# Attention over kept tokens on one core: reordering ScalarE's squares and sums, VectorE's bias and the length reductions

## The chip, the cores and the metric

The kernel runs on one core of one Trainium2 chip. The core has five engines, which run in parallel, each through its own queue in order: TensorE (PE in the profile; PEld is its weight load), VectorE (DVE), ScalarE (ACT), GpSimd (POOL) and SyncE (SP, which only issues DMAs here). Times are device microseconds (us) of whole executions; for each kernel the median of several runs is given. One further execution is profiled; its span runs from the first to the last instruction.

## The reference

A residual attention over 8 batches of 512 features by 1024 tokens in float32, with a mask of zeros and ones per token and the same projection for queries, keys and values:

```python
xt = jnp.transpose(x, (0, 2, 1))
q = xt @ Wq.T
qh = q.reshape(B, T, NH, dk).transpose(0, 2, 1, 3)          # 8 heads of 64
scores = scale * jnp.einsum('bhqd,bhkd->bhqk', qh, qh)
logits = (scores * cmask + (1.0 - cmask) * NEG) * rmask      # masked keys: NEG; masked queries: all 0
attn = jax.nn.softmax(logits, axis=-1)
ctx = jnp.einsum('bhqk,bhkd->bhqd', attn, qh)
out = x + transpose(ctx.reshape(B, T, D) @ Wo.T)
```

A masked key gets no weight, and a masked query attends to all tokens alike, so its context is the mean over tokens. About half of the tokens are kept.

## The kernel before

**What it computes on.** The kernel gathers the kept tokens of a batch (at most 543 of 1024) into 544 columns, the last of which (NK - 1) holds the mean token. Attention runs over these columns alone. Afterwards a gather by rank hands each token its row: its own, or that of the mean.

**Pairs and slots.** The order is written out by hand. The outer loop goes over 32 pairs (b, pr): batch b, and one of 4 pairs of heads. Each pair has five slots, k = 0 to 4, one for each chunk of 128 keys: first the short last chunk (64 rows, tile `el`), then chunks 0 to 3 (tile `e`). Each engine meets the work of a slot in the order in which the loop issues it:

1. scores (L584): TensorE multiplies keys by queries into `s` (PSUM, two buffers); ScalarE takes the exponential with the column `bias` of the pair (L605). The weighted values and the sums use the result.
2. add_up (L614): VectorE sums the exponentials of the chunk before, in two instructions (L622). In slot 0 also those of the pair before, then invert (reciprocals, rows out and back by SP's DMAs); in slot 4 contexts (the pair before is scaled, L740).
3. In pr 0 and 1, for the next batch: turn (VectorE transposes x, L417; SP stores it as `xd`), add_features (ScalarE sums features, L436), mean_of, search (VectorE finds the rows to gather, L473), gather (POOL's indirect DMA).
4. fetch and finish_blocks: POOL gathers output rows of the batch before into `g`; VectorE transposes a block and adds x (L825, L828). Eight blocks a batch, from pr 2 of the next batch to pr 0 of the one after; the table FINISH gives the slots, as (pr, k).
5. The list `todo[k]` of slots_of (L885): slots 0 to 2 the weighted values of the pair before (attend_short, attend_half; ScalarE copies `cT`); in pr 2, slots 1 and 2, put_mean and collect (TensorE transposes gathered tokens into `xc`); in slot 3 bias_of for the next pair and project (`pq`, `qT`) for the pair after that; in slot 4 values for the latter; in pr 1, slots 3 and 4, the output projection (`po`) of the batch before.

**The bias.** The exponentials subtract a bound on the scores. values (L543) makes the transposed values `v`, lets ScalarE square them (`sq`, L559), and VectorE adds the squares by rows (`len`, L561, 128x640) and takes the largest (`top`, L568). bias_of (L570) transposes this column on TensorE (L574), and VectorE makes `m` (L576, L577) and `bias` (L579) of it. The first exponential of a pair, that of `el` in slot 0, waits for the bias.

**Where this stands in the profiled run.** Pair (5,3) runs on TensorE from 489.72 to 504.66 us, (6,0) to 521.27, (6,1) to 553.91 (it has the output projection of batch 5), (6,2) to 570.63. The transposes L574 for the pairs (6,0), (6,1) and (6,2) start at 498.93, 515.53 and 533.43, in slot 3 of the pair before each.

Of the kernel before, what the change touches and what calls it, by code (L numbers as in the profile page):

```python
# [12 lines left out]
AF = mybir.ActivationFunctionType  # L13
ALU = mybir.AluOpType
# [291 lines left out]
def attention_of_kept_tokens(ctx, tc, x, mask, wq, wo, out, ident, wqT, woT, verdict, flag):  # L306


    nc = tc.nc
# [197 lines left out]
    def put_mean(b):  # L507

        xcs[b] = sb.tile([P, ND, NK], F32, tag="xc", name=f"xc_{b}", bufs=1)
        pm = bank(f"mean_{b}")  # L510
        for d in range(ND):
            nc.tensor.matmul(
                pm[d * Q : (d + 1) * Q, :A], within, xmeans[b][:, d, :], start=True, stop=True
            )
        nc.vector.tensor_scalar(xcs[b][:, :, NK - 1], pm[:, :A], 1.0 / T, None, ALU.mult)


    qTs, vs, tops, biases = {}, {}, {}, {}
# [24 lines left out]
    def values(pair):  # L543
        nm = "%d_%d" % pair
        qT = qTs[pair]
        v = sb.tile([P, NC, P], F32, tag="v", name=f"v_{nm}", bufs=4)
        for at, n in ((0, LAST), (LAST, 1)):
            pt = bank(f"v_{nm}_{at}")
            for i in range(n):
                c = at + i  # L550
                nc.tensor.transpose(
                    pt[:, i * P : (i + 1) * P], qT[:, c * P : (c + 1) * P], ident
                )
            nc.scalar.copy(
                v[:, at : at + n, :], pt[:, : n * P].rearrange("p (c d) -> p c d", d=P)
            )
        vs[pair] = v
        sq = sb.tile([P, NC, P], F32, tag="sq", name=f"sq_{nm}", bufs=1)
        nc.scalar.activation(sq, v, AF.Square)  # L559
        lengths = sb.tile([P, 2 * NC], F32, tag="len", name=f"len_{nm}")  # L560
        nc.vector.tensor_reduce(  # L561
            lengths,
            sq.rearrange("p c (h d) -> p (c h) d", h=2),
            axis=AX.X,
            op=ALU.add,
        )
        tops[pair] = sb.tile([P, 1], F32, tag="top", name=f"top_{nm}")
        nc.vector.tensor_reduce(tops[pair], lengths, axis=AX.X, op=ALU.max)  # L568

    def bias_of(pair):  # L570

        b, pr = pair
        pt = bank(f"top_{b}_{pr}")
        nc.tensor.transpose(pt[:, :P], tops.pop(pair).to_broadcast([P, P]), ident)  # L574
        m = sb.tile([P, 1], F32, tag="m", name=f"m_{b}_{pr}")
        nc.vector.tensor_reduce(m, pt[:, :P], axis=AX.X, op=ALU.max)  # L576
        nc.vector.tensor_scalar(m, m, -SCALE, None, ALU.mult)  # L577
        biases[pair] = sb.tile([P, NC], F32, tag="bias", name=f"bias_{b}_{pr}")
        nc.vector.tensor_scalar(biases[pair], pens[:, b, :], m, None, ALU.add)  # L579
# [222 lines left out]

    BLOCKS = range(B - 1)

    def place_blocks():

        for a in range(A):
            for j in range(A):
                nc.vector.tensor_copy(
                    block_origin[a * Q : (a + 1) * Q, :, j::A],  # L810
                    placed[j * Q : (j + 1) * Q, :, a * (NT // A) : (a + 1) * (NT // A)],
                )
# [72 lines left out]
    def slots_of(p):  # L885

        b, pr = pairs[p]
        todo = [[] for _ in range(NC)]
        before = pairs[p - 1] if 0 < p < len(pairs) - 1 else None
        behind = pairs[p + 1] if p + 1 < len(pairs) else None  # L890
        ahead = pairs[p + 2] if p + 2 < len(pairs) else None
        if before:
            todo[0].append(lambda: attend_short(before))
            for hf in range(2):
                todo[1 + hf].append(lambda hf=hf: attend_half(before, hf))
        if p == 0:
            todo[0].append(lambda: project(behind, 1))
            todo[1].append(lambda: values(behind))
        late = p == 2
        if pr == 2 and b + 1 < B:  # L900
            at = (2, 2, 2, 3, 3) if late else (1, 2, 2, 2, 2)
            todo[at[0]].append(lambda: put_mean(b + 1))
            for i in range(NC):
                todo[at[i]].append(lambda i=i: collect(b + 1, i))
        if p == ND - 1:
            todo[3].append(lambda: values(behind))
        if behind:
            todo[4 if p == ND - 1 else 3].append(lambda: bias_of(behind))
        if ahead:
            for hf in range(2):  # L910
                todo[4 if late else 3].append(lambda hf=hf: project(ahead, hf))
        if ahead and not late:
            todo[4].append(lambda: values(ahead))
        if p == ND - 1:
            for d in range(ND):
                todo[3 + d // 2].append(lambda d=d: turn_weights(woT, "wo", d))
        if pr == 1 and b > 0:
            for i in range(NC):
                todo[(3, 3, 4, 4, 4)[i]].append(lambda i=i: output(b - 1, i))
        if p + 1 == len(pairs):  # L920
            for i in range(NC):
                todo[(1, 1, 2, 3, 4)[i]].append(lambda i=i: begin_output(b, i))
        return todo
# [148 lines left out]
    def late(n):  # L1072
# [14 lines left out]
        for hf in range(2):  # L1087
            project(pairs[0], hf)
        values(pairs[0])
        project(pairs[1], 0)  # L1090
        order = [LAST, *range(LAST)]
        bias_of(pairs[0])


        TURN = [(0, 2), (0, 4), (1, 0), (1, 1)]
        SEARCH = {(1, 0): (0, 1), (1, 1): (2,), (1, 2): (3,), (1, 3): (4,)}
        LATER = {(1, 1): (0,), (1, 2): (1,), (1, 3): (2, 3), (1, 4): (4,)}

# [1 line left out]
        GATHER_LATER = {(1, 4): (0, 1, 2), (2, 0): (3,), (2, 1): (4,)}  # L1100
        FETCH = {(2, k): (k,) for k in range(NC)} | {(3, k): (NC + k,) for k in range(NT - NC)}
        FINISH = {
            (2, 3): (0,),
            (2, 4): (1,),
            (3, 0): (2,),
            (3, 1): (3,),
            (3, 2): (4,),
            (3, 3): (5,),
            (3, 4): (6,),
            (0, 1): (7,),  # L1110
        }
        FINISH_LAST = {(3, 1): (0, 1), (3, 2): (2, 3), (3, 3): (4,)}
        for p, pair in enumerate(pairs):
            b, pr = pair
            before = pairs[p - 1] if p else None
            todo = slots_of(p)
            for k, c in enumerate(order):
                scores(pair, c)
                if k:
                    add_up(pair, order[k - 1])  # L1120
                if k == 0 and before:
                    add_up(before, order[-1])
                    if p + 1 < len(pairs):
                        invert(before)
                    else:
                        inv = inverses(before)
                if p + 1 == len(pairs):
                    if k == 1:
                        spread(before, inv)
                        contexts(before)  # L1130
                elif k == 4 and before:
                    contexts(before)
                if b + 1 < B:
                    if (pr, k) in TURN:
                        turn(b + 1, TURN.index((pr, k)))
                    if pr < 2 and pr * NC + k < NN * ND:
                        add_features(b + 1, pr * NC + k)
                    if pr == 1 and k == 3:
                        mean_of(b + 1)
                    for i in (SEARCH if b else LATER).get((pr, k), ()):  # L1140
                        search(b + 1, i)
                    if pr == 0 and k == 1:
                        queries_of(b + 1)
                    for i in (GATHER if b else GATHER_LATER).get((pr, k), ()):
                        gather(b + 1, i)
                if pr == 3 and k == 0 and b + 2 < B:
                    load_batch(b + 2)
                    load_ranks(b + 2)
                if pr == 1 and k == 2 and b > 0:
                    load_rest(b - 1)  # L1150
                if b > 0:
                    for i in FETCH.get((pr, k), ()):
                        fetch(b - 1, i)
                if p == 0 and k == 1:
                    place_all()
                if p == 1 and k == 4:
                    turn_places()
                if p == 2 and k == 2:
                    place_blocks()
                for i in (FINISH if b + 1 < B or pr == 0 else FINISH_LAST).get((pr, k), ()):  # L1160
                    of = b - 2 if pr == 0 else b - 1
                    if of in BLOCKS:
                        finish_blocks(of, i)
                for task in todo[k]:
                    task()
                issue_stores()
            if p + 2 == len(pairs):
                attend_short(pair)
                for hf in range(2):
                    attend_half(pair, hf)  # L1170
# [120 lines left out]
```

## Time and profile before

| what | before |
|---|---|
| median of 3 runs | 711.64 us (704.85 to 713.55) |
| profiled execution | 708.39 us, span 706.6 us |
| TensorE busy | 645.6 us, 91% of the span |
| VectorE busy | 532.7 us, 75% |
| ScalarE busy | 377.6 us, 53% |
| GpSimd busy | 172.9 us, 24% |
| mean granted TensorE clock | 0.963 |
| chain that ended last | DVE 40%, PE 30%, DMA 14%, issue 7% |

The profile page gives busy time per engine, the costliest groups of instructions by line, and the chain of work that ended last. A group's line reads: source line, engine, operation, tiles written and read, count, busy time and mean of one, then the engine's idle time just before such instructions and what ended it. The waits view lists the same idle time by who waited for whom; the timeline lists start, duration, engine and line. Busy shares are means over stages: an engine with a modest share may still be late for a part of each batch.

### The profile page before, as it was taken

How to read it: one execution, taken by the hardware profiler on the slowest of the kernel's cores; microseconds unless marked ns; L12 is line 12 of the kernel's file. 1: busy time of each engine (PE TensorE's matmuls, PEld its weight loads, DVE VectorE, ACT ScalarE, POOL GpSimd, SP SyncE). 2: the span in 40 equal slices, each digit the busy share in tenths (PEclk: the TensorE clock that was granted, in tenths of full speed). 3: DMA queues.
4: the chain of work that ended last, by engine and by line, in shares of the span. 5: the costliest groups of instructions: out<-in, count | busy, mean ns of one | idle time of the engine just before them, and what ended most of it. 6: DMA issues, size and time to landing. Idle time of an engine off the chain costs nothing.

```text
span 706.6 us, 12031 instructions
## 1 busy us (share of the span) xinstructions
PE 645.6 (91%) x4139; PEld 385.6 (55%) x4139; DVE 532.7 (75%) x1568; ACT 377.6 (53%) x763; POOL 172.9 (24%) x222
## 2 busy tenths in 40 slices
PE   6688799999999998999999998999899999999952
PEld 5555466546655665556555654546555565544421
DVE  5268858857998599786998499875998589837761
ACT  5477447646673567446673564646664455444300
POOL 4720201054012521054011521055010530024040
PEclk9899799999999999999999998999999999999985
DMA  8444242494468744794467744795546840764256
GB/s 289 150 166 108 83 152 66 117 246 132 169 159 191 231 142 159 188 272 151 168 163 171 226 147 151 194 255 165 188 120 181 242 139 15 188 156 120 60 181 191
DMA packets 96704, 116.42 MB, mean 165 GB/s; under 512 B 10304, under 2 KB 74304, under 8 KB 96624
## 3 DMA queue, kind: packets, MB, share of 16 engines
q1 hardware_dynamic: 79552, 74.07, 39.7%
q0 software_dynamic: 12848, 39.30, 16.7%
q10 hardware_dynamic: 4224, 2.10, 1.0%
q8 instruction: 36, 0.59, 0.4%
q14 instruction: 44, 0.36, 0.2%
HBM read 72.78 MB, written 42.65 MB: 163 GB/s over the span
## 4 chain that ended last, share of the span: by engine, by line
DVE 40%; PE 30%; DMA 14%; issue 7%; ACT 3%; SPq 2%; POOL 2%; DVEq 0%; POOLq 0%
DVE junk L622 12%; PE s L601 6%; PE po L756 6%; PE pq L529 6%; PE av L638 5%; DMA od<-oc 5%; DVE xr L828 5%; DMA xin<-xd,source 4%; DVE o L825 4%; DVE junk L473 4%; DMA g<-od,block_origin 3%; SPq L425 2%; DVE cT L740 2%; DVE xt L417 2%; DMA xd<-xt 2%
## 5 line engine op out<-in xcount | busy, mean ns | idle before, releaser
L622 DVE CUSTOM_DVE_ANT_0 junk<-e,valid 128x544 f32<-128x544 f32 x256 | 184.7, 721 | 18.3 <-ACT e L605 13.0
L601 PE MATMUL s<-qT 64*128 64x272 f32 (+1 forms) x1280 | 183.2, 425 | 16.5 <-ACT el L605 14.7
L605 ACT ACTIVATE e<-s,bias 128x544 f32<-128x544 f32 x256 | 170.1, 710 | 26.1 <-PE s L601 21.8
L601 PEld LDWEIGHTS s<-qT 64*128 64x128 f32 (+1 forms) x1280 | 93.4, 177 | 91.4 <-issue 39.5
L638 PE MATMUL av<-e,v 128*64 128x272 f32 x1024 | 135.0, 407 | 0.0
L529 PE MATMUL pq<-xc,wqT 128*128 128x272 f32 x512 | 124.9, 397 | 0.0
L529 PEld LDWEIGHTS pq<-xc,wqT 128*128 128x128 f32 x512 | 97.5, 196 | 19.1 <-issue 1.1
L756 PE MATMUL po<-woT,cT 128*128 128x512 f32 (+1 forms) x448 | 105.5, 434 | 0.0
L638 PEld LDWEIGHTS av<-e,v 128*64 128x64 f32 x1024 | 69.3, 139 | 58.8 <-issue 27.1
L485 POOL DMA_INDIRECT xin<-xd,source x40 | 42.6, 1065 | 213.1 <-DVE m L577 29.6
L756 PEld LDWEIGHTS po<-woT,cT 128*128 128x128 f32 (+1 forms) x448 | 47.8, 150 | 52.7 <-issue 51.9
L536 ACT COPY qT<-pq 128x272 f32<-128x272 f32 x64 | 24.7, 385 | 80.3 <-PE pq L529 80.3
L857 POOL DMA_INDIRECT g<-od,block_origin x56 | 56.6, 1011 | 36.9 <-DMA od<-oc 19.0
L825 DVE STREAM_TRANSPOSE o<-g 128x512 f32<-128x512 f32 x56 | 39.3, 701 | 29.2 <-DMA g<-od,block_origin 29.2
L763 ACT COPY oc<-po 128x512 f32<-128x512 f32 (+1 forms) x35 | 18.3, 522 | 76.4 <-PE po L756 76.4
L661 ACT COPY cT<-av 128x272 f32<-128x272 f32 x62 | 23.9, 385 | 59.3 <-PE av L638 59.3
L561 DVE TENSOR_REDUCE len<-sq 128x10 f32<-128x640 f32 x32 | 25.9, 808 | 31.8 <-ACT sq L559 31.8
L765 POOL DMA_DIRECT2D od<-oc x56 | 30.3, 543 | 77.1 <-ACT oc L763 59.1
L381 POOL TENSOR_SCALAR valid<-count,kept 128x544 f32<-128x544 f32 x8 | 13.1, 1642 | 144.4 <-DVE sums L700 144.3
L417 DVE STREAM_TRANSPOSE xt<-x 128x1024 f32<-128x1024 f32 x28 | 34.7, 1240 | 14.9 <-DMA xd<-xt 14.3
L473 DVE TENSOR_SCALAR_CACHE_REDUCE junk<-rank,key 128x1024 f32<-128x1024 f32 (+4 forms) x40 | 39.8, 994 | 2.6 <-ACT rank L1031 2.4
L622 DVE CUSTOM_DVE_ANT_0 junk<-el,part 128x272 f32<-128x272 f32 x64 | 29.3, 457 | 15.3 <-ACT el L605 14.2
(139 smaller groups left out, 649.5 us busy)
## 6 DMA issues: line engine op xcount, KB each, us to landing
x<-in_x_dram SPq DMA_DIRECT2D x56, 256.0 KB
xd<-xt SPq DMA_DIRECT2D x112, 128.0 KB
xr<-in_x_dram SPq DMA_DIRECT2D x28, 512.0 KB
out_dram<-xr SPq DMA_DIRECT2D x24, 512.0 KB
rb<-row SPq DMA_DIRECT2D x60, 160.0 KB
od<-oc POOLq DMA_DIRECT2D x28, 256.0 KB, 7.4
rank<-ranks SPq DMA_DIRECT2D x6, 512.0 KB
xd<-xt POOLq DMA_DIRECT2D x8, 256.0 KB, 4.5
```

Source lines behind the costliest of these rows:

```text
L417: nc.vector.transpose(xt.rearrange("p k (d f) -> p k d f", d=ND), xs[b][r][:, :, at : at + n].rearrange("p d (k t) -> p k d t", t=Q),)
L473: nc.vector.tensor_scalar(junk[:, :n], rank[:, i * P :], key[:, col], 0.0, ALU.is_le, ALU.add, accum_out=found[:, col])
L485: nc.gpsimd.indirect_dma_start(out=xin[:n, :], out_offset=None, in_=xds[b], in_offset=bass.IndirectOffsetOnAxis(ap=searches[b][2][:n, i : ...
L529: nc.tensor.matmul(pq[:, :KH], wqT[:, d, pr * P : (pr + 1) * P], xcs[b][:, d, cols], start=(d == 0), stop=(d == ND - 1),)
L601: nc.tensor.matmul(s[to, h, :KH], qT[heads[h], keys], qT[heads[h], queries], start=True, stop=True)
L605: nc.scalar.activation(e[:, hf if c < LAST else 0, :, :], s[:, :, :KH], AF.Exp, bias=biases[pair][:, c : c + 1], scale=SCALE,)
L622: nc.vector.tensor_tensor_reduce(junk[:, :n].rearrange("p (f k) -> p f k", k=KH), e[:, :, h, :], (valid if c < LAST else part).rearrange(" ...
L638: nc.tensor.matmul(av[head, :KH], v[keys, c, head], e[keys, hf if c < LAST else 0, h, :], start=(c == first), stop=(c == last),)
L756: nc.tensor.matmul(po[k * n : (k + 1) * n, :w], cTs[b, pr][:, i * P : i * P + n], woT[:, pr, k * w : (k + 1) * w], start=(pr == 0), stop=( ...
L825: nc.vector.transpose(o.rearrange("p k t -> p (k t)"), gs[b, i])
L828: nc.vector.tensor_tensor(to, o, to, ALU.add)
L857: nc.gpsimd.indirect_dma_start(out=g, out_offset=None, in_=ods[b], in_offset=bass.IndirectOffsetOnAxis(ap=block_origin[:, b, i : i + 1], a ...
```

## The change

Six edits, all of order or of engine; the arithmetic stays the same.

1. put_mean writes the mean's column of `xc` on ScalarE instead of VectorE.
2. The squares, `len` and `top` leave values and become a function lengths_of. It ran with values, in slot 4 of the pair before the one that makes the bias. Now it stands in slot 1 of the pair that makes the bias in slot 3: first in todo[1], ahead of attend_half (in the first pair in slot 2, in the fourth in slot 3).
3. bias_of is issued right after the scores of slot 3 (the fourth pair: slot 4), ahead of add_up, instead of in the todo list at the end of the slot.
4. The feature sums move from one in each of the eight slots from pr 0, k 0 to pr 1, k 2 to slots 1, 2 and 3 of pr 0 and pr 1, two of them in each slot 3; mean_of moves from slot 3 to slot 4 of pr 1.
5. finish_blocks moves one slot back for blocks 0 to 6, so that block 0 comes in slot 4 of pr 2 (it was slot 3) and block 6 in slot 0 of pr 0 (it was slot 4 of pr 3).
6. place_blocks, 16 casts of a table, is cut in two halves and moves from slot 2 of the third pair to slots 0 and 1 of the fourth.

```diff
-        nc.vector.tensor_scalar(xcs[b][:, :, NK - 1], pm[:, :A], 1.0 / T, None, ALU.mult)
+        nc.scalar.mul(xcs[b][:, :, NK - 1], pm[:, :A], 1.0 / T)
...
         vs[pair] = v
+
+    def lengths_of(pair):
+
+        nm = "%d_%d" % pair
         sq = sb.tile([P, NC, P], F32, tag="sq", name=f"sq_{nm}", bufs=1)
-        nc.scalar.activation(sq, v, AF.Square)
+        nc.scalar.activation(sq, vs[pair], AF.Square)
         lengths = sb.tile([P, 2 * NC], F32, tag="len", name=f"len_{nm}")
         nc.vector.tensor_reduce(
             lengths,
...
-    def place_blocks():
-
-        for a in range(A):
+    def place_blocks(half):
+
+        for a in range(half * A // 2, (half + 1) * A // 2):
...
+        if behind:
+            if p == 0:
+                todo[2].append(lambda: lengths_of(behind))
+            elif p != ND - 1:
+                todo[1].insert(0, lambda: lengths_of(behind))
...
         if p == ND - 1:
             todo[3].append(lambda: values(behind))
-        if behind:
-            todo[4 if p == ND - 1 else 3].append(lambda: bias_of(behind))
+            todo[3].append(lambda: lengths_of(behind))
...
         values(pairs[0])
+        lengths_of(pairs[0])
...
+        FEATURES = {(r, k): (r * G + k - 1, *((r * G + 3,) if k == 3 else ())) for r in range(NN) for k in (1, 2, 3)}
...
         FINISH = {
-            (2, 3): (0,),
-            (2, 4): (1,),
-            (3, 0): (2,),
-            (3, 1): (3,),
-            (3, 2): (4,),
-            (3, 3): (5,),
-            (3, 4): (6,),
+            (2, 4): (0,),
+            (3, 0): (1,),
+            (3, 1): (2,),
+            (3, 2): (3,),
+            (3, 3): (4,),
+            (3, 4): (5,),
+            (0, 0): (6,),
             (0, 1): (7,),
         }
...
                 scores(pair, c)
+                if k == (4 if p == ND - 1 else 3) and p + 1 < len(pairs):
+                    bias_of(pairs[p + 1])
                 if k:
                     add_up(pair, order[k - 1])
...
-                    if pr < 2 and pr * NC + k < NN * ND:
-                        add_features(b + 1, pr * NC + k)
-                    if pr == 1 and k == 3:
+                    for i in FEATURES.get((pr, k), ()):
+                        add_features(b + 1, i)
+                    if pr == 1 and k == 4:
                         mean_of(b + 1)
...
-                if p == 2 and k == 2:
-                    place_blocks()
+                if p == ND - 1 and k < 2:
+                    place_blocks(k)
```

## The prediction

> **What bounds the kernel now.** I read the page's busy shares first.
>
> ```profile
> PE 645.6 (91%) x4139; PEld 385.6 (55%) x4139; DVE 532.7 (75%) x1568; ACT 377.6 (53%) x763; POOL 172.9 (24%) x222
> ```
>
> TensorE (PE) sets the pace: 91% busy, so all the idle time that a reordering can recover is small. Next the waits of TensorE, because they are that idle time by cause (columns: total us, times, longest).
>
> ```profile
> PE s L601 <- ACT el L605: 14.7, 19, 3.3
> ...
> PE av L638 <- DVE m L576: 5.0, 4, 1.3
> PE xc L498 <- DVE xc L515: 4.6, 1, 4.6
> ...
> PE s L601 <- ACT e L605: 1.8, 1, 1.8
> ...
> PE top L574 <- DVE top L568: 0.7, 1, 0.7
> ```
>
> The four upper rows are what the change aims at: 26.1 us, 3.7% of the 706.6 us span. The last row is the one to remember: the transpose `top` of bias_of hardly ever waits for VectorE (DVE) today. Then the timelines around pairs (6,0) and (6,1), TensorE first, because VectorE's mean share of 75% hides where it is late.
>
> ```profile
> 498.93 0.32 PE L574 MATMUL top<-ident,top 128*128 128x128 f32 x1
> ...
> 508.67 0.73 PE L601 MATMUL s<-qT 64*128 64x272 f32 x4 [1.86 <-ACT el L605]
> ...
> 515.53 0.32 PE L574 MATMUL top<-ident,top 128*128 128x128 f32 x1
> ...
> 523.69 0.68 PE L638 MATMUL av<-el,v 64*64 64x272 f32 x4 [1.28 <-DVE m L576]
> ...
> 533.43 0.32 PE L574 MATMUL top<-ident,top 128*128 128x128 f32 x1
> ```
>
> VectorE over the same stretch:
>
> ```profile
> 487.43 0.71 DVE L825 STREAM_TRANSPOSE o<-g 128x512 f32<-128x512 f32 x1 [5.87 <-DMA g<-od,block_origin]
> ...
> 500.93 0.69 DVE L828 TENSOR_TENSOR xr<-o,xr 128x512 f32<-128x512 f32 x1
> ...
> 512.63 0.81 DVE L561 TENSOR_REDUCE len<-sq 128x10 f32<-128x640 f32 x1
> ...
> 518.79 0.69 DVE L828 TENSOR_TENSOR xr<-o,xr 128x512 f32<-128x512 f32 x1
> ...
> 541.36 0.15 DVE L476 TENSOR_SCALAR source<-found 128x1 int32<-128x1 f32 x1
> ```
>
> VectorE stands 5.87 us for the first gathered block, and after that runs late through pairs (5,3), (6,0) and (6,1). The rows 500.93, 518.79 and 541.36 are the last thing it does for slot 1 of these pairs; they end at 501.62, 519.48 and 541.51. TensorE is by then past its transpose `top` of slot 3 (498.93, 515.53, 533.43). So VectorE's slot 1 ends 2.7, 3.9 and 8.1 us after TensorE's slot-3 `top` of the same pair. It costs little today, since len (512.63) is queued a whole pair ahead of its transpose.
>
> **The change part by part.** Gains first; the ceiling is the 26.1 us.
>
> Squares: 0.65 us from the start of sq to the next start (490.67 to 491.32), taken out between the copies of v and the exponentials of slot 0; feature sums, 0.62 us each (508.51 to 509.13), leave slots 0 and 4. In slot 1 ScalarE then has two exponentials 1.21, a sum 0.62, a square 0.65, a copy about 0.30: 2.8 us beside 3.1 us of TensorE (scores 1.12, av 1.98), so it is hidden; without that cover it costs up to 0.65 a pair. The ScalarE part of the waits goes (1.77, 1.15, 1.15, 1.18 us at 43.0, 53.5, 126.6, 444.5, and some 0.2 and 0.54 ones).
>
> Bias first: the chain m, m, bias takes 0.65 us (488.79 to 489.44) and passes two sums (1.53) and a finish (1.36) or a search. Its late arrival behind the 1.86 and 1.28 us goes. What waits for it now: VectorE itself, for the transpose; the sums behind it start later, at most the 2.7 us from 481.56 to 484.3, where it was idle anyway.
>
> Mean's column: L515 is 0.17 us on VectorE, where 2.97 us of block_origin casts stood ahead of it (80.4 to 83.4) and TensorE idled 4.63. ScalarE's nearest rows are 0.20 (a one-column read) and 0.25 (128x96); 0.2 taken, hidden by the four transposes beside it. Gain: 4.63, and a half clock after it, below. The casts move to pair (0,3), where VectorE has room (busy 4.37 of the 10 us from 92 to 102): nothing. mean_of, 0.3 us, moves one slot back and is read a pair later: nothing. The finishes one slot later cost nothing as such (8 x 1.36 either way); they take one finish off the queue ahead of a slot-1 place, and that is in the sums below. No DMA moves in its queue: the store of a finished batch is still issued after block 7 in slot 1 of pr 0, the gathers of POOL and the row stores of SP keep their slots, and the moved sums, squares and reductions issue none.
>
> **len and top a pair later.** 0.92 us (494.57 to 495.49), moved from slot 4 of the pair before to the end of slot 1, two slots ahead of the transpose on TensorE that reads it. TensorE works in order: behind that transpose stand the projections, the next scores, and in pr 1 the output matmuls. So this part turns VectorE's lateness into a TensorE wait. I count VectorE's queue in the new order, by starts in the trace: two sums 1.53, sums of el 0.84, invert 1.13, contexts 2.37, finish 1.36, turn 1.20, searches 1.36, 1.22, 1.11.
> - To len of (6,0): the bias can run at 484.3, when its transpose is done, and ends at 485.0. Then sum, sum, contexts, finish 0, sum, invert, finish 1, el, finish 2, len: 13.93, end 498.93. TensorE asks at 498.93: level.
> - To len of (6,1): sum, finish, bias, sum, finish, sum, contexts, finish, sum, invert, finish, el, finish, len: 18.8, end 517.8. TensorE, without its 1.86, asks at 513.7: it waits **4.1 us**.
> - To len of (6,2): sum, turn, bias, sum, sum, contexts, turn, sum, invert, turn, two searches, el, turn, search, len: 20.5, end 538.3; up to 1.5 more if the third turn again waits for its buffer's store (2.33 at 534.57). TensorE asked at 533.43 in the run before, with that batch's old waits (0.20, 1.86, 1.28) already in it. So the transpose comes **4.9 us later than before**: this is the net of all old waits removed and all new ones added up to here, not one wait alone. The new wait itself is 3 to 4.5, since TensorE, released at 517.8, needs some 15 us for its own work to the next transpose.
>
> The end 538.3 is 3.2 ahead of today's slot-1 end, 541.51. In batches 2 to 6 slot 1 of (b,1) ends on VectorE 9.3, 9.3, 11.2, 7.9 and 8.1 us after `top`; less 3.2 that is a net delay of 6.1, 6.1, 8.0, 4.7, 4.9, mean 6.0; with a third of the turn's wait, **6.5 us a batch**. Pair (b,1) then goes on with projections and outputs, over 18 us of pure TensorE work, and nothing gives the delay back.
>
> **The clock.** Idle TensorE has a second price (columns: us, busy of PE, PEld, DVE, ACT, POOL, granted clock, DMA, GB/s).
>
> ```profile
> 79.00:83.60 4.60, 0.00 (x0) 0.00 (x0) 4.31 (x21) 0.91 (x2) 0.00 (x0) 0.74 0.21 74
> 83.60:91.50 7.90, 7.87 (x25) 5.44 (x26) 6.90 (x22) 2.25 (x4) 0.00 (x0) 0.50 0.00 0
> ...
> 427.60:432.80 5.20, 5.14 (x22) 2.33 (x22) 4.96 (x13) 2.54 (x7) 0.00 (x0) 0.50 0.59 230
> ...
> 525.00:528.40 3.40, 3.40 (x16) 1.69 (x16) 3.23 (x9) 2.44 (x6) 0.00 (x0) 0.51 0.95 227
> ```
>
> After idle stretches of 4.63, 3.35 and 1.28 us TensorE worked 7.9, 5.2 and 3.4 us at half clock, so lost about 3.9, 2.6 and 1.7. The wait before len of (b,1) has its slow stretch swallowed by the next wait. After that of (b,2) output work follows and the loss shows: 1.7 to 3.9, taken as **2.3** for a wait of about 3 to 4.5 us.
> The Trainium skill (TensorE: Matmul & The Clock Gate, Part 1) puts the gate's return at half rate after at least one idle window of about 3.4 us, so that shorter waits would be free; here 1.28 us was enough, so the trace disagrees. By that rule the 2.3 a batch would fall away.
>
> **Sum.** Batches 2 to 6: 5 x (6.5 + 2.3) = 44. Batch 1 has turns and searches but no finishes: lag 3.4 at (1,1) (137.99 against 134.63), plus 1.7: +5. Batch 7: no turns and searches; +4 for (7,0). Batch 0: -4.6 - 3.9 for mean's column, +1 for pair (0,1) (slot 1 there ends 0.8 late): -7.5. Together +45.5: span 752, and the run, 1.8 outside the span, 754 against 708.4. The median shown, 711.64, is 3 above that profiled run; I forecast **755**.
>
> **The rivals.** Within 2% is about what a measurement here can tell from no change.
> 1. Faster: VectorE catches up. If it reaches slot 1 of (b,1) over 8 us sooner than now (over 4 in (b,0)), `top` never waits, and the 26.1 us less a few 0.2s, with the half clocks after them, go: 680 to 690, say 685. For it: 5.87 us of idle at 481.56, filled by bias and sums, and one finish less. Against it: these are in my count and give 3.2. Chance 0.12.
> 2. The waits trade places: `top` waits about as long as the exponentials do today, or the clock stays high and the delay is half: 716 (700 to 725). For it: the level result at (6,0). Against: three batches with lags over 9. Chance 0.12. That the change misses its aim on ScalarE belongs here too: a square in slot 1 holds back the copy of cT, and 5 to 10 us of the gain stays away.
> 3. Worse: VectorE gains nothing, the full lag of 9.2 plus 0.97 for len becomes the delay, with 3.9 of clock: 5 x 14 + 10 = 80, 788. Chance 0.08.
>
> Forecast (slower by 726 to 780): 0.68. Range 716 to 785: it leaves out rival 1, half of rival 2 and a little above. Faster 0.12, same 0.12, slower 0.76.
>
> **What would show it.** Right: `PE top <- DVE top` grows from 0.7 to 40 us or more, with two or three waits a batch in (b,0) and (b,1) of batches 2 to 6, the longest 3 to 7; `PE s <- ACT el` falls under 4, the 4.63 at 79.0 is gone, ScalarE's busy time is unchanged, mean clock is under 0.96. Wrong: few or short waits at `top`, because VectorE's slot 1 ends before 533 in (6,1).

## The result, and the profile after

The changed kernel takes 752.86 us (median of 4 runs, 752.26 to 755.51); the kernel before takes 710.0 (median of 4, the earlier three among them). The ratio is **1.062, 95% interval 1.054 to 1.069**: slower, and within 3 us of the forecast of 755. The profiled span grew from 706.6 to 751.3 us, by 44.7.

The page of the changed kernel, busy times, and its slices with the granted TensorE clock in tenths:

```profile
PE 658.5 (88%) x4139; PEld 399.7 (53%) x4139; DVE 532.7 (71%) x1560; ACT 375.8 (50%) x771; POOL 173.2 (23%) x222
...
PEclk9799998999889998899988998899988999999985
```

VectorE and ScalarE do the same work as before; TensorE is busy 13 us longer with the same 4139 instructions, which is the slower clock (mean 0.925, 0.963 before). The rest of the 44.7 us is waiting. The waits of TensorE in the changed kernel (total us, times, longest):

```profile
PE top L578 <- DVE top L572: 57.8, 21, 5.7
...
PE s L605 <- ACT e L609: 1.0, 1, 1.0
...
PE s L605 <- ACT el L609: 0.2, 1, 0.2
```

The wait for ScalarE and the bias is gone, almost all of it. In its place stands the row that was 0.7 us before: `top` waits 57.8 us for VectorE. TensorE's timeline around pairs (6,0), (6,1) and (6,2), the transpose alone:

```profile
532.91 0.32 PE L578 MATMUL top<-ident,top 128*128 128x128 f32 x1 [0.68 <-DVE top L572]
...
551.86 0.48 PE L578 MATMUL top<-ident,top 128*128 128x128 f32 x1 [4.69 <-DVE top L572]
...
572.73 0.48 PE L578 MATMUL top<-ident,top 128*128 128x128 f32 x1 [3.89 <-DVE top L572]
```

VectorE there:

```profile
550.79 0.81 DVE L565 TENSOR_REDUCE len<-sq 128x10 f32<-128x640 f32 x1
...
551.64 0.16 DVE L572 TENSOR_REDUCE top<-len 128x1 f32<-128x10 f32 x1
```

VectorE reaches len at 550.79, TensorE has stood since 547.17 and goes on 0.06 us after `top` ends. Between the three ends of `top` lie 18.9 and 20.9 us of VectorE's queue. The same places by stretch (us, busy PE, PEld, DVE, ACT, POOL, granted clock, DMA, GB/s):

```profile
547.20:551.90 4.70, 0.04 (x1) 0.05 (x2) 4.56 (x12) 2.21 (x6) 0.76 (x2) 0.86 0.13 34
551.90:557.40 5.50, 5.50 (x13) 4.22 (x14) 5.18 (x15) 0.39 (x1) 0.00 (x0) 0.50 0.94 235
557.40:568.80 11.40, 11.40 (x90) 6.45 (x89) 10.05 (x28) 8.64 (x19) 0.00 (x0) 1.00 0.73 181
568.80:572.70 3.90, 0.04 (x2) 0.00 (x0) 3.80 (x11) 2.28 (x6) 0.00 (x0) 0.79 0.80 222
572.70:577.90 5.20, 5.17 (x12) 3.98 (x13) 4.96 (x15) 0.39 (x1) 1.10 (x2) 0.50 0.95 229
```

In both waits VectorE is busy throughout (4.56 of 4.70 us, 3.80 of 3.90), and len has no idle time before it, so the square was ready: VectorE is behind with its queue. After each wait TensorE works 5.2 to 5.5 us at half clock.

Over a whole batch VectorE is not the slower engine. In other places it stands for TensorE and ScalarE:

```profile
DVE junk L626 <- ACT e L609: 47.0, 10, 6.6
DVE junk L626 <- ACT el L609: 43.8, 7, 6.4
DVE m L580 <- PE top L578: 39.6, 11, 5.1
```

The two engines wait for each other in turn, and no later part of the batch wins the time back.

From the first scores of pair (b,3) to those of (b+1,3) on TensorE, in us:

| from, to | before | changed | difference |
|---|---|---|---|
| start to (0,3) | 93.4 | 84.3 | -9.1 |
| (0,3) to (1,3) | 78.4 | 84.5 | +6.1 |
| (1,3) to (6,3), five batches | 398.8 | 443.7 | +44.9 |
| (6,3) to the end of the span | 136.0 | 138.8 | +2.8 |

### The profile page after: what moved, and what is told of

Same layout as the page of the kernel before. It is cut to its first block, busy times and chain, and to the rows that moved or that the text cites. A ratio compares the mean times of both kernels' runs of the same rounds, so it can differ in the third digit from the quotient of the medians.

```text
span 751.3 us, 12016 instructions
## 1 busy us (share of the span) xinstructions
PE 658.5 (88%) x4139; PEld 399.7 (53%) x4139; DVE 532.7 (71%) x1560; ACT 375.8 (50%) x771; POOL 173.2 (23%) x222
## 4 chain that ended last, share of the span: by engine, by line
PE 49%; DVE 37%; DMA 5%; issue 5%; ACT 2%; SPq 1%; POOL 1%; DVEq 0%; POOLq 0%
PE po L760 14%; DVE junk L626 10%; PE pq L529 10%; PE s L605 8%; PE av L642 7%; DVE xt L417 4%; DVE junk L473 4%; DVE o L829 3%; DVE xr L832 3%; PE xc L498 3%; DVE len L565 2%; DVE cT L744 2%; DMA xd<-xt 2%; PE pa L780 2%; DVE rb L739 2%
## 5 line engine op out<-in xcount | busy, mean ns | idle before, releaser
L609 ACT ACTIVATE e<-s,bias 128x544 f32<-128x544 f32 x256 | 168.9, 711 | 29.4 <-PE s L605 25.2
L605 PE MATMUL s<-qT 64*128 64x272 f32 (+1 forms) x1280 | 175.9, 418 | 1.3 <-ACT e L609 1.0
L529 PE MATMUL pq<-xc,wqT 128*128 128x272 f32 x512 | 153.0, 462 | 0.0
L529 PEld LDWEIGHTS pq<-xc,wqT 128*128 128x128 f32 x512 | 117.3, 235 | 28.2 <-issue 0.8
L642 PE MATMUL av<-e,v 128*64 128x272 f32 x1024 | 131.4, 399 | 0.0
L861 POOL DMA_INDIRECT g<-od,block_origin x56 | 58.4, 1043 | 33.6 <-issue 17.1
L578 PE MATMUL top<-ident,top 128*128 128x128 f32 x32 | 12.1, 379 | 58.0 <-DVE top L572 57.8
L578 PEld LDWEIGHTS top<-ident,top 128*128 128x128 f32 x32 | 4.8, 151 | 70.9 <-DVE top L572 66.8
```

Source lines behind the costliest of these rows:

```text
L529: nc.tensor.matmul(pq[:, :KH], wqT[:, d, pr * P : (pr + 1) * P], xcs[b][:, d, cols], start=(d == 0), stop=(d == ND - 1),)
L605: nc.tensor.matmul(s[to, h, :KH], qT[heads[h], keys], qT[heads[h], queries], start=True, stop=True)
L609: nc.scalar.activation(e[:, hf if c < LAST else 0, :, :], s[:, :, :KH], AF.Exp, bias=biases[pair][:, c : c + 1], scale=SCALE,)
L642: nc.tensor.matmul(av[head, :KH], v[keys, c, head], e[keys, hf if c < LAST else 0, h, :], start=(c == first), stop=(c == last),)
L861: nc.gpsimd.indirect_dma_start(out=g, out_offset=None, in_=ods[b], in_offset=bass.IndirectOffsetOnAxis(ap=block_origin[:, b, i : i + 1], a ...
```

## The experiments

Two theories. **Q**: VectorE is late in its queue, and len in slot 1 makes TensorE wait for that lateness. **V**: the early bias makes VectorE stand for TensorE, so it becomes late; len only shows it. A third question is what the half clock costs by itself.

### len back in slot 4 (e1)

```diff
         vs[pair] = v
+        lengths_of(pair)
...
-        if behind:
-            if p == 0:
-                todo[2].append(lambda: lengths_of(behind))
-            elif p != ND - 1:
-                todo[1].insert(0, lambda: lengths_of(behind))
```

(and without the two other calls of lengths_of)

> The changed kernel with one edit undone: squares, len and top run again with values, in slot 4 of the pair before; all other edits stay. Theory Q (VectorE is late in its queue, and len in slot 1 turns this into a TensorE wait): the 57.8 us that the transpose top waits for VectorE fall under 3, the half-clock stretches after them go, and with the old waits of L601 and L638 mostly gone too the time is 680 to 695 us. Theory V (the bias ahead of the sums makes VectorE stand still for TensorE, which is what makes it late; len only shows it): the lateness stays, and the time stays at 725 us or more.

Measured: 682.13 us, 0.960 of the kernel before (0.955 to 0.965). Waits of TensorE:

```profile
PE s L606 <- ACT el L610: 9.4, 19, 0.6
...
PE top L579 <- DVE top L573: 0.7, 1, 0.7
```

One edit undone turns +6% into -4%; `top` is at 0.7 us again. V is out: the bias stands ahead of the sums here too, and VectorE stands for its transposes even longer than in the changed kernel (39.6 us there), in the faster kernel:

```profile
DVE m L581 <- PE top L579: 44.1, 9, 6.7
```

What is left are waits of 0.54 us for the exponential of el, where the square stands again between the copies of v and el.

### len alone (e2)

The kernel before, with lengths_of as the changed kernel has it and nothing else.

> The kernel before with only this edit: lengths_of as in the changed kernel (slot 1 of the pair that makes the bias); bias, finishes, sums of features, mean's column and casts as before. Theory Q: VectorE's lag in batches 2 to 6 (9.2 us on average at (b,1)) counts in full, plus 0.97 for len itself, plus half clock: 765 to 790 us, slower than the changed kernel. Theory V: without the early bias nothing is lost, 705 to 720 us.

Measured: 747.79 us, 1.051 (1.046 to 1.056).

```profile
PE top L578 <- DVE top L572: 48.1, 15, 7.1
...
PE xc L498 <- DVE xc L515: 5.3, 1, 5.3
...
PE s L605 <- ACT el L609: 3.0, 8, 0.4
```

The direction is Q's: this edit alone makes the kernel slow. The size is not: 765 to 790 was expected. I had carried over the lag of the undisturbed run in full, but part of that lag was VectorE's own standing for the first gathered block, and this shrinks when TensorE is late: VectorE waits 7.7 us in all for the blocks here (first line), 29.2 in the kernel before (second).

```profile
DVE o L829 <- DMA g<-od,block_origin: 7.7, 5, 3.4
```

```profile
DVE o L825 <- DMA g<-od,block_origin: 29.2, 6, 7.6
```

The other five edits, worth 4% in e1, are worth nothing with len in slot 1: the changed kernel has 57.8 us of waits at `top`, this one 48.1. Between the len of (b,0) and that of (b,1) the new FINISH table has five finishes, the old one four; that this makes the difference was not run.

### len at the start of slot 0 (e3)

```diff
+                if k == 0 and p not in (0, ND - 1) and p + 1 < len(pairs):
+                    lengths_of(pairs[p + 1])
                 if k:
                     add_up(pair, order[k - 1])
```

(in place of the call in slot 1)

> The changed kernel with lengths_of issued right after the scores of slot 0 of the pair that makes the bias, instead of in slot 1: on VectorE ahead of the sums, invert and finish of slot 0 and all of slot 1 (6.2 us of work in (b,0), 9.6 in (b,1)), on ScalarE behind the exponential of el. Theory Q: the waits of top, at most 5.7, are shorter than what is jumped, so they vanish; 678 to 692 us, at or a few us below the kernel with len back in slot 4, since the square no longer stands between the copies of v and el. Theory V: no better than 725 us.

Measured: 690.79 us, 0.972 (0.967 to 0.976). `top` waits 2.3 us in all, as Q says. But the time is 9 us above e1, which I had expected at or below it. VectorE's waits in e3 and in e1, then TensorE's in e3:

```profile
DVE len L565 <- ACT sq L563: 55.9, 13, 14.9
```

```profile
DVE len L566 <- ACT sq L564: 22.8, 5, 12.9
```

```profile
PE av L642 <- DVE m L580: 7.9, 5, 1.7
```

len now stands at the head of VectorE's slot 0, and ScalarE makes its square only after the exponential of el. VectorE stands 55.9 us for it (22.8 in e1), and part of this comes back as a late bias, 1.5 to 1.7 us in each of batches 2 to 6. These 7.9 us are no more than the 9.4 that e1 waits for el, but three of the five waits are followed by 3.4 us at half clock, and the waits of 0.54 us in e1 by none: the mean clock is 0.963 here, 0.976 there.

### Filling the waits (e4, e5, e10)

```diff
         pt = bank(f"top_{b}_{pr}")
+        if (b > 1 and pr == 1) or (0 < b < B - 1 and pr == 2):
+            for _ in range(10):
+                nc.tensor.matmul(pt[:, P:NB], ident, woT[:, 0, P:NB], start=True, stop=True)
```

> The changed kernel with 10 matmuls of 384 columns (about 0.33 us each, 3.3 in all; their result is not used) put on TensorE ahead of the transpose top of pairs (b,1), b 2 to 7, and (b,2), b 1 to 6, where it waits 3.6 to 5.7 us. They fill idle time and shorten no wait. If the half clock after the waits costs time of its own (2.3 us a batch in the prediction): the clock stays high there and the run is 10 to 18 us faster than the changed kernel. If the waits alone make the loss: the same time, or slower by what the matmuls overrun the shorter waits, 0 to 5 us.

Measured: 747.89 us, 1.051 (1.046 to 1.056); 5 us under the changed kernel (1.051 against 1.062 by the ratios), so neither answer. The timeline shows why:

```profile
366.86 6.72 PE L580 MATMUL top<-woT,ident 128*128 128x384 f32 x20
373.42 0.27 PE L581 MATMUL top<-ident,top 128*128 128x128 f32 x1
```

Ten calls are twenty instructions and 6.6 us, twice what I had reckoned, and in batches 2 to 6 they overran the waits by 1.1 to 1.9 us. e5 has them sized: 7 calls for (b,1), 9 for (b,2), fewer in the first and last batch.

> The matmuls of the warm run again, sized to the waits this time: in e4 each call of 384 columns came out as two instructions, 0.66 us, so ten took 6.6 and overran the waits. Now 7 calls (4.6 us) ahead of top of (b,1), b 2 to 6, 5 for (7,1), 9 (5.9 us) ahead of top of (b,2), b 2 to 6, 8 for (1,2); their result is not used. If the half clock costs time of its own, 5.7 us at half rate behind the wait of (b,2), so 2.85 in each of 6 batches, and 1.5 in batch 7: 733 to 738 us against 752.9 of the changed kernel. If the 5 us of e4 were all there is: 745 to 752.

Measured: 758.34 us, but on a chip that ran the kernel before at 730.93, so the microseconds can't be compared; the ratio is 1.038 (1.031 to 1.046). To have it beside the changed kernel on one chip, both ran again:

> The changed kernel unaltered, beside the next three on one chip, since the chip of e5 to e8 ran the kernel before 19 us slower than that of e1 to e4. Its ratio to the kernel before should again be near 1.06.

> The kernel of e5 beside the changed kernel. If the half clock behind the waits of (b,2) costs time of its own: 15 to 20 us below e9. If not: within 7 us of it.

Measured: e9 754.92 us, 1.066 (1.059 to 1.073); e10 738.72 us, 1.043 (1.036 to 1.050), **16.2 us less**, within the 15 to 20 expected for a half clock with a price of its own. e10's timeline at (6,1) and (6,2), and its clock:

```profile
534.48 4.78 PE L585 MATMUL top<-woT,ident 128*128 128x384 f32 x14
539.23 0.32 PE L586 MATMUL top<-ident,top 128*128 128x128 f32 x1
553.42 6.07 PE L585 MATMUL top<-woT,ident 128*128 128x384 f32 x18
560.14 0.32 PE L586 MATMUL top<-ident,top 128*128 128x128 f32 x1 [0.65 <-DVE top L572]
```

```profile
539.30:544.80 5.50, 5.50 (x30) 4.16 (x30) 5.18 (x15) 1.79 (x5) 0.00 (x0) 1.00 0.95 229
...
560.10:565.40 5.30, 5.26 (x21) 3.92 (x22) 5.06 (x16) 0.91 (x3) 1.17 (x2) 1.00 0.91 214
```

The added matmuls don't bring `top` forward in VectorE's queue; only the clock behind the transposes is 1.00 instead of 0.50, and each of the five middle batches takes 86.2 us in the mean instead of 88.7. So idle time and slow clock are two costs, and the second is 16 of the 46 us by which e9 is slower than the kernel before. That it is the idle time that brings the half clock follows from the same pair: work in its place, even useless work, keeps the clock up.

### The other edits, each left out of e1 (e6, e7, e8)

```diff
-                if k == (4 if p == ND - 1 else 3) and p + 1 < len(pairs):
-                    bias_of(pairs[p + 1])
...
+        if behind:
+            todo[4 if p == ND - 1 else 3].append(lambda: bias_of(behind))
```

> The kernel with len back in slot 4 (682.1), and with bias_of back in the todo list, behind the sums, the finish or the search of its slot. Theory Q: the bias of (b,1) has 0.2 us to spare there and comes 2.9 us later now, so the waits of el come back with some half clock: 695 to 706 us. If VectorE were no longer late: 681 to 685.

```diff
-        nc.scalar.mul(xcs[b][:, :, NK - 1], pm[:, :A], 1.0 / T)
+        nc.vector.tensor_scalar(xcs[b][:, :, NK - 1], pm[:, :A], 1.0 / T, None, ALU.mult)
```

> The kernel with len back in slot 4 (682.1), and with mean's column on VectorE again. Only batch 0 is expected to differ: the casts are gone from ahead of it, but the column stands behind the sums of slot 2 of pair (0,2). The old wait there was 4.63 plus 3.9 of half clock, so up to 690; if the casts alone made it, 682 to 684.

```diff
-            (2, 4): (0,),
-            (3, 0): (1,),
...
+            (2, 3): (0,),
+            (2, 4): (1,),
```

(the whole FINISH table as before)

> The kernel with len back in slot 4 (682.1), and with FINISH as before (block 0 in slot 3 of pr 2). VectorE again stands for block 0, some 3 to 6 us a batch, behind the early bias, and has one finish more ahead of the bias of (b,1), which has 0.2 us to spare: 1 to 2 us a batch with its clock, 687 to 697. If the early bias alone is enough: 681 to 685.

These three ran on the chip of e5, with the kernel before at 730.93 us, so only ratios count; that ratios carry over to this chip rests on one pair of runs of the same kernel, e5 with 1.038 and e10 with 1.043. e6: 0.967 (0.959 to 0.976). e7: 0.976 (0.968 to 0.984). e8: 0.981 (0.974 to 0.987). Beside 0.960 and 0.965 for e1 and its repetition, e8's loss is clear, e7's nearly, and e6's not. By the ratios they would be 689, 695 and 698 us on the chip of e1. The 695 to 706 expected of e6 were too much; e7 lies above its 690, and e8 just above its 687 to 697. e6's trace has the bias back as a releaser, but only `PE av L643 <- DVE m L581: 3.3, 4, 1.0`; its waits for the exponential of el, 14.2 us, say nothing, since e7 and e8, which keep the early bias, have 18.6 and 21.5 on this chip. Why e8 loses is not shown: VectorE was to stand some 3 to 6 us a batch for block 0, and it waits 4.0 us in all for gathered blocks.

e7 has one place that decides it, in batch 0:

```profile
75.70:79.60 3.90, 0.00 (x0) 0.00 (x0) 3.54 (x18) 0.74 (x2) 0.00 (x0) 0.80 0.05 8
79.60:88.00 8.40, 8.35 (x32) 5.53 (x33) 4.29 (x15) 4.26 (x7) 0.00 (x0) 0.50 0.11 40
```

TensorE waits 3.96 us for mean's column, then works 8.4 us at half clock: 4.0 + 4.2 = 8.2, and pair (0,3) begins at 91.4 us there, at 83.7 in e8 on the same chip and at 82.7 in e1. So this small edit is worth some 8 us, the casts' move not counted.

### The square and the reductions apart (e11, e12)

e11 is the kernel of e1 again. e12 parts lengths_of in two:

```diff
+                if k == 0 and p not in (0, ND - 1) and p + 1 < len(pairs):
+                    squares_of(pairs[p + 1])
...
                     add_up(before, order[-1])
+                    if p != ND - 1 and p + 1 < len(pairs):
+                        lengths_of(pairs[p + 1])
```

> The kernel of e1 beside the others: ratio to the kernel before 0.955 to 0.965, about 70 us below e9.

> The changed kernel with the square and the reductions parted: the square on ScalarE right behind the exponential of el in slot 0, len and top on VectorE in slot 0 behind the sums of the pair before and ahead of invert (the first and the fourth pair as in e1). Theory Q: len is still over 6 us of queue ahead of its place in the changed kernel, so top does not wait, and the 0.54 us waits of L601 for el (9.4 us in e1), which come from the square between the copies of v and el, go: 3 to 9 us below e11. If VectorE stands for the square as it did in e3 (55.9 us idle there), it comes out between e11 and e3's ratio, 0.972.

Measured: e11 683.79 us, 0.965 (0.960 to 0.971); e12 681.82 us, 0.962 (0.955 to 0.968): 2 us less, inside both intervals, and less than the 3 to 9 expected.

```profile
PE top L585 <- DVE top L579: 5.4, 6, 0.9
...
PE av L649 <- DVE m L587: 3.7, 5, 0.9
```

The 0.54 us waits for el are gone, as meant, and 9.1 us of waits at `top` and for the bias have come for them. len now stands behind the sums of the pair before, 1.5 us of queue later than in e11, and there `top` had 0.5 us to spare at (6,2) (it ends at 506.63, the transpose starts at 507.10): VectorE is just too late again. The five batches from (1,3) to (6,3) take 383 us in both. That VectorE stands for the square, the other outcome considered, is true too, but not what costs:

```profile
DVE len L572 <- ACT sq L565: 46.2, 10, 14.8
```

In batches 2 to 6 these waits, 2.3 to 3.1 us, all fall on the len made for the pairs (b,3), whose `top` is done some 8 us before TensorE asks for it.

## Why the prediction was right

**The cause.** `top` grew from 0.7 to 57.8 us; 40 or more was named, with a longest wait of 3 to 7 us (it is 5.7). The other marks hold too: the wait for el is 0.2 us (under 4), ScalarE's busy time is 375.8 us against 377.6, the mean clock is 0.925 (under 0.96). e1 and e2 show from both sides that the move of len decides. Rival 1 (VectorE catches up) needed `top` never to wait, and at (6,2) it waits 3.89 us. Rival 2 needed waits no longer than those of today for the exponentials, 14.7 us in all, or a clock that stays high; neither came. Rival 3 had 14 us a batch from the full lag and the clock; a batch came out 9.0 us longer.

**The sums along VectorE's queue.** The count gave a level result at (6,0); the wait is 0.68 us. It gave 4.1 us at (6,1), measured 4.69, and 3 to 4.5 us at (6,2), measured 3.89. Between the ends of `top` it had 18.8 and 20.5 us of queue; they are 18.9 and 20.9. The counting was done on instructions that all stood in the trace, and only their order was new.

**Batches.** For batches 2 to 6 the prediction had 44 us; they came out at 44.9. Batch 1 had +5 and came out at +6.1, batch 0 had -7.5 and came out at -9.1, the end had +4 and came out at +2.8. That the sum, 45.5, is within a microsecond of 44.7 owes something to these misses cancelling. Within the five batches too: each takes 88.5 to 88.9 us in the changed kernel, 76.9 to 82.6 in the kernel before, and the single differences are up to 2.7 us off what was counted.

**The clock.** The prediction took 2.3 us a batch behind the wait of (b,2). By the rows it is 5.2 us at half rate, so 2.6; by the batches of e9 and e10 (88.7 and 86.2) it is 2.5. The Trainium skill (TensorE: Matmul & The Clock Gate, Part 1) has the clock fall to half after an idle window of about 3.4 us. The waits at (b,1) and (b,2) of batches 2 to 6, 3.6 to 4.7 us, fit it, so the changed kernel doesn't test the prediction's objection, and its remark that by this rule the 2.3 would fall away holds only for waits below 3.4. Shorter waits brought the half clock as well: 1.28 us at 522.4 in the kernel before, 2.58 us at 196.6 and 282.6 in e2 (half clock from 200.3 and 285.7). But "1.28 us was enough" is not a rule either: the same 1.28 us at 360.2 and 1.86 us at 506.8 in the kernel before, and 2.58 us at 369.8 in e2, were followed by none. First the kernel before at 360.2 and at 522.4, then e2 at 196.6 and at 369.8 (columns as above):

```profile
357.70:361.11 3.41, 2.51 (x25) 1.30 (x21) 3.34 (x8) 3.24 (x9) 0.00 (x0) 1.00 0.63 189
361.11:364.53 3.42, 3.04 (x22) 1.57 (x24) 3.19 (x13) 2.80 (x7) 0.00 (x0) 1.00 0.94 211
521.54:524.95 3.41, 2.13 (x20) 0.79 (x13) 3.27 (x11) 2.76 (x8) 0.00 (x0) 1.00 0.94 247
524.95:528.36 3.41, 3.41 (x16) 1.74 (x16) 3.24 (x9) 2.48 (x6) 0.00 (x0) 0.50 0.96 228
```

```profile
196.92:200.34 3.42, 1.14 (x6) 0.98 (x7) 3.32 (x7) 1.22 (x4) 0.00 (x0) 1.00 0.15 48
200.34:203.75 3.41, 3.41 (x9) 2.58 (x8) 3.31 (x11) 0.39 (x1) 0.00 (x0) 0.50 0.92 254
367.61:371.02 3.41, 2.21 (x18) 1.11 (x14) 3.24 (x11) 2.62 (x7) 2.04 (x3) 1.00 0.01 2
371.02:374.43 3.41, 2.03 (x10) 1.72 (x11) 3.34 (x8) 0.32 (x2) 0.00 (x0) 1.00 0.46 124
```

The half-clock stretches here last 3.41 us each, and the rows are cut in steps of that length, in each run counted from where its half clock begins. The waits that brought it lie almost whole in the step ahead of it; the waits of equal length that didn't are split between two steps. Where a wait falls thus seems to count beside its length. No run tests this, and the busy time of the step alone doesn't settle it (2.13 us of 3.41 was followed by the half clock, 2.03 in e2 was not).

**The gains.** e1 shows how much of the ceiling of 26.1 us the edits reach with len in its old place, some 15 us: the scores' wait for ScalarE falls from 16.5 to 11.2, that for the bias from 5.0 to 0.2, and mean's 4.6 is gone. That the span of e1 is 26.4 us shorter all the same is the clock again, mean 0.976 against 0.963: TensorE is idle 14.2 us less and busy 12.2 us less with the same instructions.

**Where I was wrong** is in what followed: e2's size (a lag taken from an undisturbed run, though part of it was a wait that shrinks), e3's place against e1 (a square on ScalarE that VectorE stands for, and the half clock behind it), e12's gain (the 1.5 us by which len moved back), e4's filling (two instructions a call) and e6.

Left open: why the chip of e5 to e8 ran everything some 3% slower. Its profiles show waits of 1 to 2 us of TensorE for `qT` behind the projection `pq` (2.04 at 168.9 in e7, 0.3 in all in e1), and longer ones for the exponentials, that the others don't have. What held ScalarE there they don't tell: ahead of that copy of `qT` in e7 it stands 5.00 us for nothing that the core's engines show.

## What to carry to other kernels

Before moving a producer later, read off the trace where its engine really is when the consumer asks, not in which slot the code puts it: an engine that is busy 75% on average can be 8 us behind in the stretch that counts. Then add up its queue in the new order from the durations at hand; here that gave the three waits counted to within 0.7 us. And count the half clock as a second price of TensorE waits of a few microseconds: here it was 16 of 46 us.

## What the runs showed of the hardware

- Filling TensorE's idle time with useless matmuls made the kernel 16.2 us faster (738.72 against 754.92): a wait at full clock is cheaper than a wait that lets the clock fall.
- The half clock behind a wait came in stretches of 3.41 us or two or three times that. Of waits of equal length (1.28 us in the kernel before, 2.58 in e2) some brought it and some didn't.
- A float32 matmul of 128x128 by 384 columns is two instructions and 0.66 us at full clock (e4).
- The same kernel before ran at medians of 710.0, 711.95, 730.93 and 708.51 us in the four comparisons: microseconds are for one chip, ratios for several.
